# Bilinear blending of a deformable convolution: from rows-then-columns to columns-then-rows, with ScalarE first

## The chip, the core and the metric

The kernel runs on one core of a Trainium2 chip. The metric is the device time of one execution in microseconds (us), and the comparison is of medians. TensorE (PE) multiplies and transposes, its weight loads are listed as PEld; VectorE (DVE) and ScalarE (ACT) work element by element; GpSimd (POOL) issues the gathers; SyncE (SP) issues the other transfers. Each engine takes its own instructions strictly in the order in which they were written for it, and waits for others by semaphores.

## What is computed

The input is x, 4 images of 256 channels of 64 x 64 pixels, in float32. Three deformable 3 x 3 convolutions with ReLU follow each other on a normalised x, the result is added to x, and a mixture of eight experts (two per token) works on the pixels as tokens. The change is in the sampling of the deformable convolution, in the reference:

```
v00 = _gather(feat, y0i, x0i); v01 = _gather(feat, y0i, x1i)
v10 = _gather(feat, y1i, x0i); v11 = _gather(feat, y1i, x1i)
return v00*(1-wy)*(1-wx) + v01*(1-wy)*wx + v10*wy*(1-wx) + v11*wy*wx
...
sampled = _bilinear(x, ys, xs) * mask[:, None]
out = jnp.einsum('bikhw,oik->bohw', sampled, wk) + b[None, :, None, None]
```

Every output pixel takes, for each of 9 taps, four neighbouring pixels (two rows, a left and a right column) of 256 channels, blends them with weights of its own, and multiplies by a 256 x 256 matrix of that tap.

## The kernel before

A table in HBM holds for each position 512 values: the 256 channels of the upper pixel (v) and the 256 differences from it to the lower pixel (d). So `v + wy*d` blends two rows, and two neighbouring positions lie next to each other: one gather of 1024 values per pixel brings the left column (v, d) and the right column (v, d).

The work goes in 12 stages (3 layers x 4 images, interleaved), each of 8 blocks of 512 pixels, each block in 9 taps, each tap in four tiles of 128 pixels: 12 x 8 x 9 x 4 = 3456 tiles. `main_block` (L430) does for each tile:

- gather `g` (L445, POOL), into a ring of `GB` = 10 buffers of 4 KB a partition;
- **D1** (L451, DVE, 512 values): `g.v += wy * g.d`, for both columns, in place;
- **A** (L456, ACT, 256 values): `s = left * cf[1]`, with `s` from a ring of 6;
- **D2** (L461, DVE, 256 values): `s += right * cf[2]`;
- **T** (L465, PE): two transposes of `s` into PSUM. When the two tiles of a pair are transposed, **S** (L470, ACT) copies the pair to `sT`.

In the source the pair is written D1, A, D1, A, D2, D2. After the four tiles, `finish` (L477) issues the products of the tap before (L488, PE, from its `sT`), `step` and `pump` (L870) hand out pieces of other work: storing the table of the next layer (L263), the offset convolution and its plan of positions (L310), normalising (L388), and routing and experts of images that are done (L519 to L842).

The order of instructions on each engine isn't the source's: a scheduler sorts them when the program is built, by its own estimate of what is ready when. Within an engine the order is then fixed. A buffer of `g` is free again when its last reader is done (here D2); the gather that takes it waits for that on POOL, in front of all later gathers.

Of the kernel before, what the change touches and what calls it, by code (L numbers as in the profile page):

```python
# [8 lines left out]
F32 = mybir.dt.float32  # L9
I32 = mybir.dt.int32  # L10
AF = mybir.ActivationFunctionType
ALU = mybir.AluOpType
AX = mybir.AxisListType

P = 128
H = W = 64
C = 256
CC = C // P
K = 9
# [15 lines left out]
FT_LOG = 8  # L35
FT = 1 << FT_LOG
FU = FT // P
GB = 10
WINN = CC * (RPB + 2) * (W + 2)
W1N = CC * HID + HC  # L40
W2N = HC * C + C
# [43 lines left out]
class Weave:  # L85
# [3 lines left out]
    def __init__(self, ctx, tc, ins, out):  # L89
# [7 lines left out]
        def pool(name, bufs, **kw):  # L97
            return ctx.enter_context(tc.tile_pool(name=name, bufs=bufs, **kw))
# [14 lines left out]
        self.smp = pool("smp", 6)  # L113
        self.gat = pool("gat", GB)
        self.ps = pool("ps", 3, space=bass.MemoryType.PSUM)
# [314 lines left out]
    def main_block(self, i, n, wins):  # L430
        nc = self.nc
        l, b = self.stages[i]
        nm = f"{i}_{n}"
        idx, cf = self.plans.pop((l, b, n))
        tb = self.table(l, b)
        acc = self.ps1.tile([P, CC, BLK], F32, tag="acc", name=f"acc_{nm}")
        for k in range(K):
            sT = self.smT.tile([P, CC, BLK], F32, tag="sT", name=f"sT_{nm}_{k}")
            for t0 in range(0, TPB, 2):
                tp = self.ps.tile([P, CC, 2 * P], F32, tag="tp", name=f"tp_{nm}_{k}_{t0}")  # L440
                gs, ss = [], []
                for t in (t0, t0 + 1):
                    j = t * K + k
                    g = self.gat.tile([P, 2, 2, C], F32, tag="g", name=f"g_{nm}_{j}")
                    nc.gpsimd.indirect_dma_start(  # L445
                        out=g.rearrange("p x s f -> p (x s f)"),
                        out_offset=None,
                        in_=tb,
                        in_offset=bass.IndirectOffsetOnAxis(ap=idx[:, j : j + 1], axis=0),
                    )  # L450
                    nc.vector.scalar_tensor_tensor(  # L451
                        g[:, :, 0, :], g[:, :, 1, :], cf[:, j, 0:1], g[:, :, 0, :],
                        ALU.mult, ALU.add,
                    )
                    s = self.smp.tile([P, C], F32, tag="s", name=f"s_{nm}_{j}")
                    nc.scalar.activation(s, g[:, 0, 0, :], AF.Copy, scale=cf[:, j, 1:2])  # L456
                    gs.append(g)
                    ss.append(s)
                for u in range(2):
                    j = (t0 + u) * K + k  # L460
                    nc.vector.scalar_tensor_tensor(  # L461
                        ss[u], gs[u][:, 1, 0, :], cf[:, j, 2:3], ss[u], ALU.mult, ALU.add
                    )
                    for c in range(CC):
                        nc.tensor.transpose(  # L465
                            tp[:, c, u * P : (u + 1) * P],
                            ss[u][:, c * P : (c + 1) * P],
                            self.ident,
                        )
                nc.scalar.copy(sT[:, :, t0 * P : (t0 + 2) * P], tp)  # L470

            self.finish()
            self.pend = (i, n, k, acc, sT, wins)
            self.step(k)
            self.pump()
# [501 lines left out]
```

## Time and profile before

| | us |
|---|---|
| median of 17 runs | 8086.85 (8047.05 to 8119.2) |
| the profiled execution | 8099.05 |
| its span, first to last instruction | 8097.1 |
| PE busy | 6793.9 (84%) |
| DVE busy | 5034.7 (62%) |
| POOL busy | 4519.1 (56%) |
| ACT busy | 3581.9 (44%) |
| transfers of gathered and other indirect data | 1929.26 MB |
| read from HBM and written | 290 GB/s over the span |

The mean granted clock of TensorE is 0.932 of full speed. The first 170 us make the first table (the first gather is at 166.6 us), the convolutions run until about 7515 us, and the last 580 us are experts and sums of the last image. PE's busy time includes overlap that the profile models, so it is not PE at its peak.

In a list of instructions a row gives start, duration, engine, line, operation, result and sources, how many were merged, and in brackets the idle time of the engine before it and what ended it. In a list of waits a row gives the waiting instruction, what it waited for, and the total in us, how many times, the longest. In a table of stretches a row gives, for each of PE, PEld, DVE, ACT and POOL, busy us and instructions, then granted clock, busy share of the DMA engines and GB/s.

### The profile page before, as it was taken

To read this page: it belongs to the slowest core of one execution; us is meant where nothing else is said; L and a number is where in the kernel's file an instruction comes from. 1 tells how busy PE (TensorE), PEld (TensorE's weight loads), DVE (VectorE), ACT (ScalarE), POOL (GpSimd) and SP (SyncE) were. 2 spreads that over 40 slices of the span, in tenths; PEclk is the share of its full clock that TensorE was granted. 3 is DMA by queue.
4 is the path that set the end of the run, shared out by engine and by line. 5 is a ranking of instruction groups with operands and counts; after the bars stand their busy time and mean duration, and the time that the engine had idled before them with its cause. 6 is when DMAs were issued, how large, how long until landed. Compare 5 with 4: busy or idle time off the path is not lost. (4 is left out here: it accounts for less than half of the span.)

```text
span 8097.1 us, 92242 instructions
## 1 busy us (share of the span) xinstructions
PE 6793.9 (84%) x27544; PEld 3720.1 (46%) x27544; DVE 5034.7 (62%) x11300; ACT 3581.9 (44%) x7355; POOL 4519.1 (56%) x4189
## 2 busy tenths in 40 slices
PE   6898888888988989988877899988887787778595
PEld 2444333334444444445533445544444444445374
DVE  4776777778885666666667666666665544556401
ACT  3554544445544444445543444444543333444121
POOL 1665666665655666655555566655555544545434
PEclk8999999999999999999988999999998889889697
DMA  5998999899987888887778888888787666667423
GB/s 154 324 329 283 335 328 320 311 326 335 349 290 275 307 298 302 299 283 276 284 270 277 277 304 294 305 294 288 272 296 233 237 231 223 245 239 276 139 94 117
DMA packets 751193, 2210.66 MB, mean 273 GB/s; under 512 B 105688, under 2 KB 206040, under 8 KB 746088
## 3 DMA queue, kind: packets, MB, share of 16 engines
q0 software_dynamic: 547392, 1929.26, 68.0%
q1 hardware_dynamic: 203304, 275.51, 10.1%
q8 instruction: 222, 3.64, 0.2%
q14 instruction: 275, 2.25, 0.1%
HBM read 2150.57 MB, written 195.61 MB: 290 GB/s over the span
## 5 line engine op out<-in xcount | busy, mean ns | idle before, releaser
L445 POOL DMA_INDIRECT g<-tab,idx x3456 | 3735.8, 1081 | 2474.8 <-DVE s L461 1274.9
L488 PE MATMUL acc<-sT,wk 128*128 128x512 f32 x6912 | 3503.8, 626 | 286.2 <-ACT sT L470 161.8
L461 DVE SCALAR_TENSOR_TENSOR s<-g,cf,s 128x256 f32<-128x256 f32 x3456 | 1625.0, 482 | 1751.0 <-ACT s L456 1306.3
L451 DVE SCALAR_TENSOR_TENSOR g<-g,cf 128x512 f32<-128x512 f32 x3456 | 2520.6, 745 | 235.1 <-DMA g<-tab,idx 193.9
L456 ACT ACTIVATE s<-g,cf 128x256 f32<-128x256 f32 x3456 | 1691.1, 509 | 1172.9 <-DVE g L451 895.6
L488 PEld LDWEIGHTS acc<-sT,wk 128*128 128x128 f32 x6912 | 1218.5, 199 | 1298.8 <-issue 940.5
L470 ACT COPY sT<-tp 128x512 f32<-128x512 f32 x1728 | 1002.4, 584 | 1747.2 <-PE tp L465 1196.3
L465 PE MATMUL tp<-ident,s 128*128 128x128 f32 x6912 | 1306.1, 287 | 427.8 <-DVE s L461 280.0
L465 PEld LDWEIGHTS tp<-ident,s 128*128 128x128 f32 x6912 | 878.9, 146 | 1664.5 <-issue 1014.5
L791 PE MATMUL py<-w,hT 128*128 128x256 f32 x2496 | 693.5, 400 | 139.0 <-ACT hT L785 99.9
L775 PE MATMUL ph<-fzT,w 128*128 128x256 f32 x2496 | 675.1, 401 | 68.0 <-ACT hT L785 26.4
L791 PEld LDWEIGHTS py<-w,hT 128*128 128x128 f32 x2496 | 449.6, 196 | 288.2 <-ACT hT L785 150.2
L727 POOL DMA_INDIRECT w<-in_W,wrow x156 | 174.8, 1121 | 723.7 <-issue 292.4
L775 PEld LDWEIGHTS ph<-fzT,w 128*128 128x128 f32 x2496 | 470.7, 200 | 195.8 <-issue 85.2
L321 PE MATMUL po<-win,wo 128*32 128x512 f32 x2304 | 469.1, 617 | 53.1 <-ACT win L256 31.3
L785 ACT ACTIVATE hT<-ph,w 128x256 f32<-128x256 f32 x624 | 268.3, 471 | 547.4 <-PE ph L775 285.2
L739 POOL DMA_INDIRECT zt<-z,tok x312 | 348.3, 1116 | 140.7 <-issue 87.2
L820 POOL DMA_INDIRECT gy<-ys,slots x256 | 258.9, 1011 | 228.4 <-DVE ta L828 117.2
L799 DVE TENSOR_TENSOR y<-py,w 128x512 f32<-128x512 f32 x156 | 107.5, 689 | 345.7 <-PE py L791 315.4
L291 ACT COPY hv<-tpv 128x512 f32<-128x512 f32 x384 | 211.1, 595 | 110.3 <-PE tpv L286 54.1
L321 PE MATMUL po<-win_pre,wo 128*32 128x512 f32 x1152 | 228.0, 632 | 19.0 <-ACT om L330 7.5
L828 DVE SCALAR_TENSOR_TENSOR ta<-gy,cw,ta 128x256 f32<-128x256 f32 x256 | 121.0, 483 | 121.6 <-DMA gy<-ys,slots 80.6
(151 smaller groups left out, 3644.8 us busy)
## 6 DMA issues: line engine op xcount, KB each, us to landing
tab<-hv SPq DMA_DIRECT2D x384, 256.0 KB
g<-tab,idx POOLq DMA_INDIRECT x3456
ys<-y SPq DMA_DIRECT2D x156, 256.0 KB
wk<-in_conv_w SPq DMA_DIRECT2D x108, 256.0 KB
xc_pre<-in_x SPq DMA_DIRECT2D x32, 512.0 KB
xr_tok<-in_x SPq DMA_DIRECT2D x32, 512.0 KB
t<-t_tok SPq DMA_DIRECT2D x32, 512.0 KB
ta<-t SPq DMA_DIRECT2D x64, 256.0 KB
```

What stands on the lines that cost most here:

```text
L321: nc.tensor.matmul(po[g * Q : (g + 1) * Q, :], lhsT=self.wo[l][:, k, c, :], rhs=w[:, c, ky : ky + RPB, kx : kx + W], start=(m < NQ), stop= ...
L445: nc.gpsimd.indirect_dma_start(out=g.rearrange("p x s f -> p (x s f)"), out_offset=None, in_=tb, in_offset=bass.IndirectOffsetOnAxis(ap=id ...
L451: nc.vector.scalar_tensor_tensor(g[:, :, 0, :], g[:, :, 1, :], cf[:, j, 0:1], g[:, :, 0, :], ALU.mult, ALU.add,)
L456: nc.scalar.activation(s, g[:, 0, 0, :], AF.Copy, scale=cf[:, j, 1:2])
L461: nc.vector.scalar_tensor_tensor(ss[u], gs[u][:, 1, 0, :], cf[:, j, 2:3], ss[u], ALU.mult, ALU.add)
L465: nc.tensor.transpose(tp[:, c, u * P : (u + 1) * P], ss[u][:, c * P : (c + 1) * P], self.ident,)
L470: nc.scalar.copy(sT[:, :, t0 * P : (t0 + 2) * P], tp)
L488: nc.tensor.matmul(acc[:, o, :], lhsT=self.wk[k][:, c, o * P : (o + 1) * P], rhs=sT[:, c, :], start=(k == 0 and c == 0), stop=(k == K - 1 ...
L739: self.nc.gpsimd.indirect_dma_start(out=zt, out_offset=None, in_=grp.zd, in_offset=bass.IndirectOffsetOnAxis(ap=grp.tok[:, j : j + 1], axi ...
L775: nc.tensor.matmul(ph[:, h, :], lhsT=w1[:, o : o + P], rhs=zT[:, c, :], start=(c == 0), stop=(c == CC - 1),)
L785: nc.scalar.activation(ht[:, h, :], ph[:, h, :], AF.Gelu, bias=w1[:, k : k + 1])
L791: nc.tensor.matmul(py[:, u, :], lhsT=hT[h // 2][:, h % 2, u * P : (u + 1) * P], rhs=w2[:, h * C : (h + 1) * C], start=(h == 0), stop=(h == ...
```

## The change

The order of blending is turned around. ACT scales the whole left column (v and d, 512 values) straight from the gathered data. DVE adds the right column (512 values) and then, directly on its own result, blends the rows (256 values). Per tile there are still one ACT and two DVE instructions. The order in the source is now A, D1, D2 for one tile, then for the next. `s` has 512 values a partition in place of 256 (6 buffers of 2 KB in place of 1 KB), and `GB` goes from 10 to 9. The last reader of `g` is now D1. The gather, the transposes, the copies and the products are the same.

```diff
-GB = 10
+GB = 9
...
-                gs, ss = [], []
-                for t in (t0, t0 + 1):
-                    j = t * K + k
-                    g = self.gat.tile([P, 2, 2, C], F32, tag="g", name=f"g_{nm}_{j}")
+                for u in range(2):
+                    j = (t0 + u) * K + k
+                    g = self.gat.tile([P, 2, 2 * C], F32, tag="g", name=f"g_{nm}_{j}")
...
+                    s = self.smp.tile([P, 2 * C], F32, tag="s", name=f"s_{nm}_{j}")
+                    nc.scalar.activation(s, g[:, 0, :], AF.Copy, scale=cf[:, j, 1:2])
                     nc.vector.scalar_tensor_tensor(
-                        g[:, :, 0, :], g[:, :, 1, :], cf[:, j, 0:1], g[:, :, 0, :],
-                        ALU.mult, ALU.add,
+                        s, g[:, 1, :], cf[:, j, 2:3], s, ALU.mult, ALU.add
                     )
-                    s = self.smp.tile([P, C], F32, tag="s", name=f"s_{nm}_{j}")
-                    nc.scalar.activation(s, g[:, 0, 0, :], AF.Copy, scale=cf[:, j, 1:2])
-                    gs.append(g)
-                    ss.append(s)
-                for u in range(2):
-                    j = (t0 + u) * K + k
                     nc.vector.scalar_tensor_tensor(
-                        ss[u], gs[u][:, 1, 0, :], cf[:, j, 2:3], ss[u], ALU.mult, ALU.add
+                        s[:, :C], s[:, C:], cf[:, j, 0:1], s[:, :C], ALU.mult, ALU.add
                     )
```

More of the change, by code (lines that the diff above doesn't have):

```diff
@@ L440, in main_block @@
                 tp = self.ps.tile([P, CC, 2 * P], F32, tag="tp", name=f"tp_{nm}_{k}_{t0}")
-                gs, ss = [], []
-                for t in (t0, t0 + 1):
-                    j = t * K + k
-                    g = self.gat.tile([P, 2, 2, C], F32, tag="g", name=f"g_{nm}_{j}")
+                for u in range(2):
+                    j = (t0 + u) * K + k
+                    g = self.gat.tile([P, 2, 2 * C], F32, tag="g", name=f"g_{nm}_{j}")
                     nc.gpsimd.indirect_dma_start(
-                        out=g.rearrange("p x s f -> p (x s f)"),
+                        out=g.rearrange("p x f -> p (x f)"),
                         out_offset=None,
@@ L465, in main_block @@
                         nc.tensor.transpose(
-                            tp[:, c, u * P : (u + 1) * P],
-                            ss[u][:, c * P : (c + 1) * P],
-                            self.ident,
+                            tp[:, c, u * P : (u + 1) * P], s[:, c * P : (c + 1) * P], self.ident
                         )
```

## Prediction

> **What bounds the kernel now.** I read the page's busy times first: PE 84%, DVE 62%, ACT 44%, so PE is nearest to the end, though not at it. The table of stretches tells whether that holds everywhere. A row of the early convolutions and one of the stages with experts beside them:
>
> ```profile
> 800.00:1200.00 400.00, 344.02 (x1341) 157.66 (x1342) 291.99 (x582) 199.63 (x412) 259.52 (x236) 1.00 0.93 330
> 4800.00:5200.00 400.00, 369.26 (x1494) 202.13 (x1493) 257.09 (x522) 188.86 (x400) 251.29 (x227) 0.97 0.84 292
> ```
>
> PE is 86% and 92% busy, DVE 73% and 64%, the DMA engines 93% and 84%. No resource is full; the rest is engines waiting for each other in turn. The list of waits says who:
>
> ```profile
> DVE s L461 <- ACT s L456: 1306.3, 1254, 15.9
> POOL g L445 <- DVE s L461: 1274.9, 1036, 10.3
> ACT sT L470 <- PE tp L465: 1196.3, 952, 6.2
> ACT s L456 <- DVE g L451: 895.6, 910, 8.7
> ...
> PEld tp L465 <- DVE s L461: 372.3, 547, 6.5
> ...
> DVE g L451 <- DMA g<-tab,idx: 193.9, 103, 9.1
> ```
>
> DVE waits for A, A for D1, the copy S for the transposes T, T for D2, and gathers for a free buffer. D1 seldom waits for data: 103 times in 3456, so gathers are ahead of their use. The durations of the ring come from the list of instructions. Early on, with one tile after the other:
>
> ```profile
> 999.80 0.48 DVE L461 SCALAR_TENSOR_TENSOR s<-g,cf,s 128x256 f32<-128x256 f32 x1
> ...
> 1000.20 0.74 DVE L451 SCALAR_TENSOR_TENSOR g<-g,cf 128x512 f32<-128x512 f32 x1
> ...
> 1000.98 0.51 ACT L456 ACTIVATE s<-g,cf 128x256 f32<-128x256 f32 x1 [1.22 <-DVE g L451]
> ...
> 1001.52 0.48 DVE L461 SCALAR_TENSOR_TENSOR s<-g,cf,s 128x256 f32<-128x256 f32 x1 [0.58 <-ACT s L456]
> ```
>
> From D2 to the next D1 0.40 us, D1 to A 0.78, A to D2 0.54: 1.72 us a tile, 3.44 a pair, in strict turns, with DVE idle 0.58 of it. Elsewhere the copy is in the way:
>
> ```profile
> 3001.56 0.49 DVE L461 SCALAR_TENSOR_TENSOR s<-g,cf,s 128x256 f32<-128x256 f32 x1 [0.58 <-ACT s L456]
> 3001.97 1.41 DVE L451 SCALAR_TENSOR_TENSOR g<-g,cf 128x512 f32<-128x512 f32 x2
> ...
> 3002.11 0.44 PE L465 MATMUL tp<-ident,s 128*128 128x128 f32 x2 [0.42 <-DVE s L461]
> ...
> 3002.58 0.58 ACT L470 COPY sT<-tp 128x512 f32<-128x512 f32 x1 [1.05 <-issue]
> 3003.06 0.91 ACT L456 ACTIVATE s<-g,cf 128x256 f32<-128x256 f32 x2
> ...
> 3003.61 0.88 DVE L461 SCALAR_TENSOR_TENSOR s<-g,cf,s 128x256 f32<-128x256 f32 x2 [0.23 <-ACT s L456]
> ```
>
> D2 to T 0.55, T to S 0.47, S to the next A 0.48, a second A 0.40 behind (0.91 - 0.51), A to D2 0.55. Both D1 ran meanwhile (second 0.67 behind the first, 1.41 - 0.74). So this pair took 0.55 + 0.47 + 0.48 + 0.40 + 0.55 = 2.45 us, and its D1 cost nothing.
>
> How much of the time is this ring? I followed the chain of waits back, by the page's rule, from a point every 130 us between 740 and 7510 us: it covers 6656 us, of which PE has 3749, D1 276, A 218, D2 204, S 123. Those four are 821 us. With some 35 us of handovers (about 700 of them at 0.05) and 75 us of transposes between D2 and S (160 at 0.47), about **930 us** of the path is the ring. The rest is mostly PE.
>
> **The change, part by part.**
>
> *ACT.* 3456 A of 256 become 512 values. The trace has no such A from SBUF. Biased ACTIVATEs from PSUM take 687 ns for 512 (L330) and 471 for 256 (L785), 216 more; plain copies of 512 take 584. Bounds: 584 and 725 (509 + 216). I take 0.72 us, since the form is an ACTIVATE: 3456 x 0.21 = 726 us more on ACT, 3582 to some 4310 (53%). Beside PE this is hidden; in the ring it counts.
>
> *DVE.* D1 and D2 keep sizes and forms (745 and 482 ns), so busy time stays near 5035. But D2 now waits for D1 on its own engine. Independent instructions overlap: D2 to D1 is 0.40 though D2 lasts 0.48. Dependent ones don't:
>
> ```profile
> 1011.99 0.20 DVE L363 TENSOR_SCALAR pos<-pos 128x72 f32<-128x72 f32 x1
> ...
> 1012.23 0.27 DVE L365 CAST pi<-pos 128x72 int32<-128x72 f32 x1
> ```
>
> The second starts 0.04 after the first has ended. So D1 to D2 is 0.745 + 0.04 = 0.79 us, and not 0.67: DVE alone needs 2 x (0.79 + 0.40) = 2.38 us a pair, before 2 x (0.67 + 0.40) = 2.14. The Trainium skill, "VectorE: DVE Perf Modes", section "The DRAIN you can't avoid", speaks otherwise: chaining with semaphores took the same time as without, so the semaphore costs nothing extra. By it, D1 to D2 stays 0.67, and the ring reckoned below would be 2.74 us a pair in place of 2.92; the rows here overlap only where nothing is awaited, so I keep 0.79.
>
> *The ring.* Before, D1 ran ahead of A whenever ACT was held up by S. Now D1 and D2 both stand behind A. What matters is how many of a pair's A stand in ACT's fixed order before the S of the pair before. I counted it in the orders of both builds (1727 pairs). Before: none 865, one 701, both 161. After: none 162, one 931, both 634. So the scheduler moves A ahead by about one tile.
>
> Before, by DVE's order as well: 643 pairs with both A behind S and both D1 ahead of D2, 2.45 us; 482 in strict turns, 3.44; the other 602 held by DVE alone, 2.14. Mean: (1575 + 1658 + 1288) / 1727 = **2.62 us a pair**.
> After, with one A behind S: D2 to T 0.55, S 0.47, A 0.48, D1 0.76 (0.72 + 0.04), D2 0.79: 3.05. With both behind, 0.40 + 0.79 more: 4.24. With none, DVE alone: 2.38. Mean: (931 x 3.05 + 162 x 4.24 + 634 x 2.38) / 1727 = **2.92 us a pair**, 11.5% more.
>
> The strict turns go, which is the change's gain, but the longer way behind each S outweighs it. If the ring set the pace throughout, that would be 1727 x 0.30 = 518 us; at the 930 us that it holds of the path, 930 x 0.115 = **107 us**. I take the latter, since PE holds 56% of the path. The lower end is a gain, priced as the first rival.
>
> *Buffers.* One gather fewer ahead is one tile's period, about 2.1 us (7340 us / 3456), whenever the reserve runs out, at most 103 times: 216 us. Against it, `g` comes free at D1 in place of D2, so below zero is possible by up to 0.79 us at the same 103 times, -81. I take **20 us**, nearer to zero, because the two partly cancel. POOL has the same 3456 gathers; behind a gather that waits stand further gathers, expert weights (L727) and token rows (L739), and behind these PE's products of L775 and L791.
>
> *PE, S, SP.* The same instructions; their places change with the scheduler. On PE the transposes of single tiles lie more evenly among the products (9592 runs of equal instructions in place of 9373). I price it at nothing: PE has work to do meanwhile. Should that cover fail, each of 1727 pairs could wait one more transpose pair, 0.2 us: up to 345 us.
>
> **Sum.** 8099 + 107 + 20 = 8226 for the profiled execution. The median stands 12 us below that execution, so I forecast **8214 us**, 1.6% slower.
>
> **The rivals.**
> 1. *Faster: the handover was the pace.* DVE's 1306 us of waiting for A vanish, because A needs landed data alone and gathers are ahead. For it: strict turns make 1.72 us a tile, and the tiles of 740 to 1740 us come every 1.70 to 1.77. Price: at least the 136 steps from D1 to A on the walked path at 0.55, 75 us; at most all 218 us of A and these 75, 293. Middle -184: 7903; span 7794 to 8012. It decides when A stays two tiles ahead of S nearly always, so that DVE runs through. Against it: in the built order that holds for 634 of 1727 pairs.
> 2. *Slower throughout: the ring sets the pace.* Most pairs have exactly one A ahead, each then takes 3.05 us, and PE's idle time grows in the stages with experts too. Price 518 us: 8605 by the median. Against it: those stages need over 4 us a pair already (8097 us / 1727 = 4.7), mostly PE's.
> 3. *No change.* PE and the transfers (93% busy early on) hide both sides: 8087. It needs a balance within 16 us.
>
> **How the numbers follow.** Forecast 0.47 (8103 to 8450), rival 1 0.32 and a smaller gain within it, rival 2 0.12, rival 3 0.09. A measurement of this kernel can tell about 0.2%, 16 us, from no change. So faster 0.32, same 0.09, slower 0.59. The range leaves out the far half of rival 1, below 7900, and most of rival 2, above 8480: **7900 to 8480**. The forecast's own range is 8103 to 8450.
>
> **What would show it.** A at 0.70 to 0.74 us, and ACT near 4310 busy; outside that the ACT step is wrong. "DVE <- ACT" at D1 should remain a long wait, 1000 us or more; under rival 1 it falls below 400. S waiting for T should grow with DVE between; D2 starts 0.79 after D1, or 0.67 if the skill's rule holds. D1 or A waiting for gathers should stay under 300 us in all; much more means that the tenth buffer mattered. A walked path with less of D1, A, D2 than 700 us makes the ring step wrong.

## The result, and the profile after the change

The changed kernel takes 8273.08 us (median of 8 runs, 8261.46 to 8295.28) against 8086.97 us (47 runs): a ratio of **1.0237 [1.0222, 1.0252]**, 186 us slower. The forecast was 8214 us.

The profiled execution spans 8262.4 us (before: 8097.1), at a mean granted clock of 0.927 (before: 0.932). The page's busy times:

```profile
PE 6811.8 (82%) x27544; PEld 3723.9 (45%) x27544; DVE 5142.6 (62%) x11300; ACT 4204.3 (51%) x7355; POOL 4403.9 (53%) x4189
```

ACT has 622 us more work and DVE 108 us more; PE has the same work and is idle for longer. The table of stretches, in the columns and the two places that the prediction shows:

```profile
800.00:1200.00 400.00, 327.85 (x1278) 149.59 (x1279) 286.90 (x555) 230.88 (x398) 238.27 (x228) 1.00 0.89 315
4800.00:5200.00 400.00, 351.33 (x1379) 186.67 (x1377) 249.19 (x481) 209.31 (x372) 221.41 (x215) 0.95 0.82 281
```

In 400 us PE does 1278 matmuls in place of 1341 early, and 1379 in place of 1494 in the stage with experts beside it: 5% and 8% less, at nearly the same clock. The same stretch of time doesn't hold quite the same work in the two kernels, so these shares overstate the loss; but it is not in the early stages alone. Cut at the first copy S of a stage and at the end of the last S, the profiled executions give (us):

| | stages 1 to 4 | stages 5 to 12 | after the last S |
|---|---|---|---|
| before | 2084 | 5257 | 581 |
| after | 2121 | 5387 | 579 |
| difference | +37 (1.8%) | +130 (2.5%) | -2 |

The experts' first products come at 2453 us in the kernel before and at 2501 in the changed one, in stage 5. The list of waits of the changed kernel (D1 is now L453, A L452, D2 L456, T L460, S L463):

```profile
ACT sT L463 <- PE tp L460: 1492.2, 1047, 6.7
DVE s L453 <- ACT s L452: 1430.3, 804, 20.9
POOL g L444 <- DVE s L453: 1430.1, 846, 8.6
...
PEld tp L460 <- DVE s L456: 527.2, 647, 6.3
...
ACT s L452 <- DMA g<-tab,idx: 185.8, 111, 9.2
...
DVE s L453 <- DMA g<-tab,idx: 109.1, 29, 8.9
```

The wait of D2 for A (1306.3) has become a wait of D1 for A (1430.3), seldomer and longer; the wait of A for D1 (895.6) is gone. In their place S waits longer for the transposes (1196.3 to 1492.2), and the weight loads of the transposes for D2 (372.3 to 527.2). What these waits look like can be read in a piece of the list of instructions:

```profile
1008.64 0.38 PE L460 MATMUL tp<-ident,s 128*128 128x128 f32 x2
...
1009.22 0.59 ACT L463 COPY sT<-tp 128x512 f32<-128x512 f32 x1 [2.58 <-PE tp L460]
...
1009.70 1.34 ACT L452 ACTIVATE s<-g,cf 128x512 f32<-128x512 f32 x2
...
1010.46 0.75 DVE L453 SCALAR_TENSOR_TENSOR s<-g,cf,s 128x512 f32<-128x512 f32 x1 [2.50 <-ACT s L452]
...
1011.25 0.48 DVE L456 SCALAR_TENSOR_TENSOR s<-s,cf 128x256 f32<-128x256 f32 x1
...
1011.65 0.75 DVE L453 SCALAR_TENSOR_TENSOR s<-g,cf,s 128x512 f32<-128x512 f32 x1
...
1011.79 0.44 PE L460 MATMUL tp<-ident,s 128*128 128x128 f32 x2
...
1012.26 0.58 ACT L463 COPY sT<-tp 128x512 f32<-128x512 f32 x1 [1.23 <-PE tp L460]
```

ACT stands 2.58 us in front of S, with two A queued behind it (the second tile of the next pair and the first tile of the pair after that), though neither then waits for its gathered data: their gathers were issued some 15 us earlier. DVE, which needs the first A, has nothing to do for 2.50 us; then come D1, D2 (0.79 behind D1), T and the next S: 3.04 us from S to S. That is the prediction's ring with an A behind S, 3.05 us.

### The profile page after: what moved, and what is told of

Same layout as the page of the kernel before. It is cut to its first block, busy times and chain, and to the rows that moved or that the text cites. A ratio compares the mean times of both kernels' runs of the same rounds, so it can differ in the third digit from the quotient of the medians.

```text
span 8262.4 us, 93641 instructions
## 1 busy us (share of the span) xinstructions
PE 6811.8 (82%) x27544; PEld 3723.9 (45%) x27544; DVE 5142.6 (62%) x11300; ACT 4204.3 (51%) x7355; POOL 4403.9 (53%) x4189
## 5 line engine op out<-in xcount | busy, mean ns | idle before, releaser
L444 POOL DMA_INDIRECT g<-tab,idx x3456 | 3650.6, 1056 | 2753.8 <-DVE s L453 1430.1
L453 DVE SCALAR_TENSOR_TENSOR s<-g,cf,s 128x512 f32<-128x512 f32 x3456 | 2559.0, 748 | 1983.7 <-ACT s L452 1430.3
L481 PE MATMUL acc<-sT,wk 128*128 128x512 f32 x6912 | 3553.4, 629 | 280.3 <-ACT sT L463 168.4
L452 ACT ACTIVATE s<-g,cf 128x512 f32<-128x512 f32 x3456 | 2354.7, 721 | 311.1 <-DMA g<-tab,idx 185.8
L463 ACT COPY sT<-tp 128x512 f32<-128x512 f32 x1728 | 1008.2, 585 | 2119.7 <-PE tp L460 1492.2
L481 PEld LDWEIGHTS acc<-sT,wk 128*128 128x128 f32 x6912 | 1217.1, 201 | 1199.1 <-issue 836.7
L460 PE MATMUL tp<-ident,s 128*128 128x128 f32 x6912 | 1346.4, 288 | 454.8 <-DVE s L456 307.9
L456 DVE SCALAR_TENSOR_TENSOR s<-s,cf 128x256 f32<-128x256 f32 x3456 | 1638.7, 482 | 108.7 <-issue 31.8
L460 PEld LDWEIGHTS tp<-ident,s 128*128 128x128 f32 x6912 | 888.2, 146 | 1807.1 <-issue 930.2
L732 POOL DMA_INDIRECT zt<-z,tok x312 | 327.7, 1050 | 140.1 <-issue 89.6
L827 PE MATMUL otp<-ident,ta 128*128 128x128 f32 x256 | 70.8, 377 | 185.9 <-issue 121.9
```

Source lines behind the costliest of these rows:

```text
L444: nc.gpsimd.indirect_dma_start(out=g.rearrange("p x f -> p (x f)"), out_offset=None, in_=tb, in_offset=bass.IndirectOffsetOnAxis(ap=idx[:, ...
L452: nc.scalar.activation(s, g[:, 0, :], AF.Copy, scale=cf[:, j, 1:2])
L453: nc.vector.scalar_tensor_tensor(s, g[:, 1, :], cf[:, j, 2:3], s, ALU.mult, ALU.add)
L456: nc.vector.scalar_tensor_tensor(s[:, :C], s[:, C:], cf[:, j, 0:1], s[:, :C], ALU.mult, ALU.add)
L460: nc.tensor.transpose(tp[:, c, u * P : (u + 1) * P], s[:, c * P : (c + 1) * P], self.ident)
L481: nc.tensor.matmul(acc[:, o, :], lhsT=self.wk[k][:, c, o * P : (o + 1) * P], rhs=sT[:, c, :], start=(k == 0 and c == 0), stop=(k == K - 1 ...
```

## The experiments

The theories at the start. **Ring**: A stands behind S in ACT's fixed order, and D1 and D2 both behind A; the place of A decides. **Long A**: ACT's 512 values by themselves cost the time. **Buffers**: the tenth gather buffer is missed. The runs came in three visits, and the kernel before took 7965, 7487 and 8076 us there; so each ratio is to the kernel before of the same visit, and ratios of different visits are compared with care.

"Pairs with both A ahead" means, as in the prediction, that both A of a pair stand in ACT's order before the S of the pair before: 161 of 1727 in the kernel before, 634 in the changed one.

### First visit: each suspect alone

**The kernel before with nine buffers.**

```diff
-GB = 10
+GB = 9
```

> The kernel before with 9 gather buffers in place of 10, nothing else. Before is 8087 us, after 8273. Ring theory (the loss is D1 standing behind A, behind the copy S): the tenth buffer is worth little, 8080 to 8130. Buffer theory (the loss is the shorter reserve of gathers): 8190 to 8270. Long-A theory (the loss is ACT's 726 us more): 8087, plus or minus 15.

Measured: 7896.24 us, **0.9925 [0.9896, 0.9953]**. No theory had the sign: nine buffers are better than ten in the old order. Its list of waits, to be read against the lines of before in the prediction:

```profile
...
DVE s L461 <- ACT s L456: 1186.7, 1279, 18.4
...
DVE g L451 <- DMA g<-tab,idx: 193.8, 133, 8.8
```

D1 waits for gathered data 193.8 us with nine buffers and, in the profile of the first result, 193.9 with ten: by this view the tenth bought no data. Why nine are faster is open; the order on the engines is nearly the same (161 pairs with both A ahead become 159). So the lost buffer does no harm in the old order. The changed kernel with ten buffers was not run, so for the new order this isn't shown.

**The same, with a long A.** ACT scales 512 values of `g`, of which the second half is not used.

```diff
-GB = 10
+GB = 9
...
-                    s = self.smp.tile([P, C], F32, tag="s", name=f"s_{nm}_{j}")
-                    nc.scalar.activation(s, g[:, 0, 0, :], AF.Copy, scale=cf[:, j, 1:2])
+                    s = self.smp.tile([P, 2 * C], F32, tag="s", name=f"s_{nm}_{j}")
+                    nc.scalar.activation(s, g[:, 0, :, :].rearrange("p s f -> p (s f)"), AF.Copy, scale=cf[:, j, 1:2])
...
```

> The kernel before with 9 gather buffers, and A over the left column's 512 values (blended values and differences; the second half of s isn't used), so A is as long as after the change, but D1 still stands ahead of A. Ring theory: A of 0.72 us costs only where A is on the ring, 0.21 us on some 471 pieces of the walked path at most, up to 100 us: 8090 to 8190. Long-A theory: all of the loss, 8250 to 8290. Buffer theory: as with 9 buffers alone, 8190 to 8270.

Measured: 7946.14 us, **0.9983 [0.9959, 1.0006]**, below every expectation, but 0.6% above the run before, which has the same nine buffers and an A of 256 values. The group of A shows that the work was there:

```profile
L456 ACT ACTIVATE s<-g,cf 128x512 f32<-128x512 f32 x3456 | 2406.7, 722 | 782.6 <-DVE g L451 428.3 <-issue 223.4 <-ACT s L456 56.7
```

A is busy 2406.7 us, in the run before 1693.3: 713 us more on ACT cost about 50 us of the kernel, where the order of D1, A, D2 is the old one. That is a net figure, since the scheduler also moved A: 1319 of 1727 pairs have at least one A ahead of S, 860 in the run before (both ahead: 214 and 159). By the ring theory that helps, so the long A by itself may cost more. In the old order it is far from the whole loss; for the new order this run says nothing.

**The new order with a short A.** ACT scales v of the left column alone, D1 works in place on `g` and adds that to both halves, and D2 blends; `g` is then held until D2, with ten buffers. This kernel leaves out the left column's differences, so its values, and with them the positions that the second and third layer gather and the choice of experts, aren't those of the other kernels. The diff is against the changed kernel.

```diff
-GB = 9
+GB = 10
...
-                    nc.scalar.activation(s, g[:, 0, :], AF.Copy, scale=cf[:, j, 1:2])
+                    nc.scalar.activation(s, g[:, 0, :C], AF.Copy, scale=cf[:, j, 1:2])
                     nc.vector.scalar_tensor_tensor(
-                        s, g[:, 1, :], cf[:, j, 2:3], s, ALU.mult, ALU.add
+                        g[:, 1, :].rearrange("p (s f) -> p s f", s=2),
+                        g[:, 1, :].rearrange("p (s f) -> p s f", s=2),
+                        cf[:, j, 2:3], s.unsqueeze(1).to_broadcast([P, 2, C]),
+                        ALU.mult, ALU.add,
                     )
                     nc.vector.scalar_tensor_tensor(
-                        s[:, :C], s[:, C:], cf[:, j, 0:1], s[:, :C], ALU.mult, ALU.add
+                        s, g[:, 1, C:], cf[:, j, 0:1], g[:, 1, :C], ALU.mult, ALU.add
                     )
```

> The new order with a short A: A scales 256 values (the left column's differences are left out), D1 adds the right column's 512 values to it in place in g, D2 blends the rows from g into s. 10 buffers, s of 256. So D1 stands behind A, but A is short and the buffers are as before. Ring theory: one A behind the copy gives 2.84 us a pair in place of 3.05, most of the loss stays: 8170 to 8260. Long-A theory and buffer theory: the loss is gone, 8070 to 8120.

Measured: 8362.96 us, **1.0504 [1.0464, 1.0544]**. Long A and buffers both wanted this kernel near the old time, and it is the slowest of all. The ring theory had the sign and missed the size. What is late is again the way from A to S:

```profile
ACT sT L466 <- PE tp L463: 1879.1, 1050, 7.6
DVE g L453 <- ACT s L452: 1315.2, 859, 13.7
```

With 508 pairs with both A ahead, in place of 634, it stands further back by the ring's measure, though its A is shorter. That goes with the loss, but isn't isolated: the longer hold of `g`, the write in place and the other positions came with it.

**The changed kernel, with A put ahead of S.** An edge that orders without a semaphore tells the scheduler to issue S only after both A of the next pair (within a block of pixels). Nothing else in the source changes.

```diff
+        held = None
...
+                scaled = []
...
-                    nc.scalar.activation(s, g[:, 0, :], AF.Copy, scale=cf[:, j, 1:2])
+                    scaled.append(
+                        nc.scalar.activation(s, g[:, 0, :], AF.Copy, scale=cf[:, j, 1:2]).ins
+                    )
...
-                nc.scalar.copy(sT[:, :, t0 * P : (t0 + 2) * P], tp)
+                if held is not None:
+                    for a in scaled:
+                        self.tc.add_manual_dep(
+                            held,
+                            a.name,
+                            mybir.DependencyInfo(
+                                mybir.DependencyClass.NoSync, mybir.DependencyReason.DATA
+                            ),
+                            reason="scale ahead of the copy",
+                        )
+                held = nc.scalar.copy(sT[:, :, t0 * P : (t0 + 2) * P], tp).ins
```

> The kernel after, with an edge for the scheduler alone (no wait on the chip): on ACT the copy S of a pair is issued after both A of the next pair in the block. 1643 of 1727 pairs then have both A ahead (634 before the edge). Ring theory: a pair falls from 2.92 to some 2.4 us, 18% of the 964 us that the ring now holds of the walked path, 170 us: 8050 to 8150. Long-A and buffer theories: nothing changes, 8260 to 8290, since ACT has the same work and the buffers are the same.

Measured: 7986.10 us, **1.0025 [1.0006, 1.0045]**, with 1643 pairs with both A ahead. That is inside the range of the ring theory. The buffers, the long A and the instructions are those of the changed kernel, and the time is nearly that of before: the place of A in ACT's order, with what the scheduler moves along with it, is worth about 2%. It does move more: 1789 of PE's 27544 instructions stand over 20 places from where they stood in the changed kernel, and 606 of DVE's 11300 over three places. No run separates these moves from the place of A. The changed kernel itself was not run in that visit, so it was taken up again below.

### Second visit: the edge in other kernels

**The changed kernel again**, with no edit.

> The kernel after, unchanged, for the same chip as the next ones, since times differ from chip to chip by over 1%. All theories: a ratio to the kernel before of 1.020 to 1.028, as measured first (1.0237).

Measured: 7558.96 us, **1.0089 [1.0070, 1.0107]**, well under the first ratio and the expectation. Here everything was faster (before 7487.41). The last section shows what was different.

**The short A with the edge**: the edit of the short A and that of the edge together, ten buffers.

> The new order with the short A (left column's differences left out, 10 buffers, g held until D2), which was 1.050 times the time before, now with both A of the next pair issued ahead of S (1640 of 1727 pairs, 508 without the edge). Ring theory: a pair then goes at DVE's own 2.38 us, whatever A's length, so the ratio is that of the same edge with the long A (1.0025): 0.995 to 1.012. If instead the excess of the short A is in its buffers (g held longer, written in place), the edge leaves at least 1.02.

Measured: 7237.47 us, **0.9672 [0.9656, 0.9688]**, below every expectation. The ring theory held that the length of A no longer matters once both A stand ahead of S. But with the long A the same edge gives 1.0025 in the first visit and 1.0011 in the third, over 3% more. So either the long A has a price in the new order that the missing edge hides, or the tenth buffer, the write in place or the left-out part of the blend has it. Other positions aren't the whole of it: in the four stages of the first layer, whose positions come from x alone, this kernel takes 2019 us and the changed kernel of this visit 2171. Which of the rest it is, no run shows.

**The short A with nine buffers**, without the edge. The diff is against the first kernel with the short A.

```diff
-GB = 10
+GB = 9
```

> The new order with the short A, 9 gather buffers in place of 10, no edge. In the old order the ninth instead of the tenth buffer gave 0.9925. If buffers explain why the short A is slower than the long one (10 against 9), 1.02 to 1.03; if they have no part in it, 1.04 to 1.055.

Measured: 7601.64 us, **1.0159 [1.0140, 1.0178]**, below both ranges. They were reckoned from ratios of the first visit, and the changed kernel fell in this one too (1.0237 to 1.0089), so what the ninth or tenth buffer does here stays open. The run is 0.6% above the changed kernel of this visit: a shorter A doesn't help while it stands behind S (506 pairs with both ahead). Between this run and the one before it lie the edge and one buffer, and 364 us.

**The kernel before with the edge**: `scaled` and `held` as above, ten buffers.

> The kernel before (old order, 10 buffers) with the same edge: on ACT, S of a pair after both A of the next pair (1634 of 1727 pairs, 161 without). Ring theory: D1 then has to stand ahead of S as well; a pair falls from 2.62 to some 2.2 us, 15% of some 930 us on the path, 140 us: ratio 0.975 to 0.99, which would beat both kernels. If A behind S isn't what costs time, 1.00 or more, because S is delayed by A.

Measured: 7395.53 us, **0.9877 [0.9854, 0.9899]**, as the ring theory had it. The old order has A behind S too, and gains from the same remedy. The edge is thus not a remedy for the change alone, and what it gives back to the changed kernel is not all the change's own loss.

### Third visit: the few tenths, on one chip

**The kernel before again**, with no edit.

> The kernel before, unchanged, for a profile on the same chip as the next three. All theories: a ratio of 1.00.

Measured: 8070.62 us, **0.9990 [0.9973, 1.0007]**: what a kernel without a difference gives.

**The changed kernel again.**

> The kernel after, unchanged, on that chip. Two chips gave 1.0237 and 1.0089. Where the waits that the profile puts down to nothing (issue) are as long as in the first two profiles, some 1.02 to 1.028; where they are short, 1.006 to 1.012.

Measured: 8251.32 us, **1.0215 [1.0200, 1.0231]**: the first result stands.

**The changed kernel with the edge again.**

> The kernel after with S held behind both A of the next pair, now beside the kernel after on one chip. Ring theory: 1.5% to 4% below the kernel after, and D1's waits for A below it too. If ACT's longer work were the cost, no more than 0.5% below the kernel after.

Measured: 8081.67 us, **1.0011 [0.9998, 1.0024]**: 170 us less than without the edge, on the same chip. Its list of waits:

```profile
...
ACT sT L477 <- PE tp L464: 1002.9, 732, 6.4
DVE s L457 <- ACT s L455: 993.7, 461, 20.1
...
PEld tp L464 <- DVE s L460: 288.9, 516, 5.1
```

Without the edge these waits were 1544.6, 1497.2 and 552.8 us in this visit; all three steps of the ring shrink together. In the list of instructions at the same place as above:

```profile
1004.24 0.59 ACT L477 COPY sT<-tp 128x512 f32<-128x512 f32 x1 [0.60 <-PE tp L464]
1004.40 0.49 DVE L460 SCALAR_TENSOR_TENSOR s<-s,cf 128x256 f32<-128x256 f32 x1
...
1004.72 1.33 ACT L455 ACTIVATE s<-g,cf 128x512 f32<-128x512 f32 x2
1004.80 0.75 DVE L457 SCALAR_TENSOR_TENSOR s<-g,cf,s 128x512 f32<-128x512 f32 x1
...
1005.59 0.48 DVE L460 SCALAR_TENSOR_TENSOR s<-s,cf 128x256 f32<-128x256 f32 x1
...
1005.99 0.75 DVE L457 SCALAR_TENSOR_TENSOR s<-g,cf,s 128x512 f32<-128x512 f32 x1
```

DVE starts D1 at 1004.80, while the two A behind S have only begun (1004.72): it works on a tile scaled before S. From D1 to D1 1.19 us, and no row of DVE has an idle time before it.

**The kernel before with the edge and nine buffers.**

> The kernel before with the same edge and 9 buffers. The edge alone gave 0.9877, 9 buffers alone 0.9925, on different chips. If the two add, 0.975 to 0.985; it should then beat both kernels. In the old order D1 must now run ahead of S on a second round trip between ACT and DVE, so ring theory expects the new order with the edge to come out at least level with it.

Measured: 7911.83 us, **0.9788 [0.9771, 0.9805]**: 2.1% faster than the kernel before, and it beats both kernels. That the new order with the edge would come out at least level with it was wrong: the new order takes 2.1% longer (8081.67 against 7911.83), with the edge and nine buffers in both. In the new order with the edge S still waits 1002.9 us for the transposes. In the old one that wait has nearly gone, but A, which stands ahead of S there, waits for D1 instead:

```profile
ACT s L459 <- DVE g L453: 1556.4, 1598, 8.7
...
ACT sT L484 <- PE tp L469: 193.7, 186, 4.7
```

The stages of the profiled executions of this visit:

| us | stages 1 to 4 | stages 5 to 12 |
|---|---|---|
| before | 2079 | 5260 |
| after | 2126 | 5404 |
| after, with the edge | 2017 | 5280 |
| before, with the edge and nine buffers | 2043 | 5088 |

In the first four stages the new order with the edge is the fastest of all, 26 us below the old one with the edge. It loses its 192 us in the stages that have experts beside them. These are single executions: that of the kernel before is 28 us above its median, that of the changed kernel 34 above, that with the edge 26 below and that of the last row 24 below.

## Why the prediction was right, and where it wasn't

The sign was right, and the way that the prediction named is there: D1, D2 and T stand behind A, A stands behind S, and with A put ahead of S 170 of 175 us went on one chip (8251 to 8082, the kernel before 8076). That does not make the place of A the whole of what divides the two orders. The same edge takes 1.2% off the old order too, and with the edge and nine buffers in both the new order still takes 2.1% longer. The prediction compared the orders mostly by the place of A. For pairs with both A ahead it has 2.38 us against 2.14 where DVE alone sets the pace, since D2 waits for D1; whether that is what is left, no run isolates. And that 8214 lies only 59 us below the measured 8273 is in part luck, since one of its two terms had the wrong sign where it was measured. By its own steps:

*ACT.* Predicted 0.72 us for A and 4310 us busy. Measured, in the groups of instructions:

```profile
L453 DVE SCALAR_TENSOR_TENSOR s<-g,cf,s 128x512 f32<-128x512 f32 x3456 | 2559.0, 748 | 1983.7 <-ACT s L452 1430.3 <-issue 288.0 <-DMA g<-tab,idx 109.1
L452 ACT ACTIVATE s<-g,cf 128x512 f32<-128x512 f32 x3456 | 2354.7, 721 | 311.1 <-DMA g<-tab,idx 185.8 <-PE tp L460 85.7 <-issue 26.1
L456 DVE SCALAR_TENSOR_TENSOR s<-s,cf 128x256 f32<-128x256 f32 x3456 | 1638.7, 482 | 108.7 <-issue 31.8 <-DMA g<-tab,idx 5.1 <-DVE s L453 3.9
```

721 ns, right. ACT is busy 4204 us in place of 4310. 62 us of that come from A that follow each other and overlap (two take 1.34 us, not 1.44), the rest lies in ACT's other work. The prediction priced the work beside PE at nothing; the long A in the old order cost about 50 us net, and with the edge the kernel with the short A is over 3% below that with the long one, for a reason that is not isolated.

*DVE.* D1 and D2 keep their durations (748 and 482 ns); DVE is busy 5143 us in place of 5035. A D2 that directly follows the D1 of its own tile starts 0.786 us after it (median of 1940); one that directly follows the D1 of another tile starts 0.662 us after it (332, in the same trace). Predicted 0.79. So the wait of an instruction for the one ahead of it on its own engine takes away the overlap, 0.12 us a tile. The Trainium skill, "VectorE: DVE Perf Modes", section "The DRAIN you can't avoid", reports that a row of eight copies took as long with a semaphore after each as without. That doesn't carry over to this pair, and the prediction read the section as wider than it is. It also says that a next instruction that isn't held starts earlier, which agrees with the 0.662 us here. What these 0.12 us cost the kernel was not isolated.

*The ring.* Its parts were right: D1 starts 0.76 us after A where it waits for it (predicted 0.76), the next D1 0.401 after D2 (0.40), and the stretch shown above takes 3.04 us from S to S (3.05). D1, A, D2 and S grew on the walked path as foreseen, from 821 to some 960 us (in the third visit from 810 to 931, and 738 with the edge); D1, A and D2 have over 800 of it, above the 700 below which the step would have been wrong. But **107 us was too little, and the reason given against more was wrong.** The prediction held that the stages with experts would hardly feel the ring, since a pair takes over 4 us there and mostly by PE's work. They lost 2.5%, more than the early ones (1.8%), and with the edge the profiled executions got back 124 us there and 109 in the early ones. The walked path doesn't show that. Behind 2240 us the four steps take some 570 us of it before and as much after (in the third visit 577 and 583), while between 740 and 2240 us they grow from 251 to 352, in stages that lost 37. Under which name the late loss stands on the path is open: issue grew (616 to 676 us in the third visit, and 593 with the edge), and the products of L481 grew in the first profiles (1361 to 1417) but not in the third visit (1367 and 1365). So the share of the path places the loss badly, though its sum came near.

*Buffers.* Predicted +20 us, for a tenth buffer that is missed at D1's waits for data. In the old order nine buffers made it 0.75% faster. In the changed kernel A and D1 wait for gathers 295 us in all (185.8 + 109.1), under the 300 set as a limit; before it was 234 (193.9 + 39.9), so the 61 us between are the most that this view gives a missed buffer. The term had the wrong sign in the only place where it was measured; if the same held in the new order, the rest of the change would cost 250 us, not 186. That is not shown.

*PE.* Priced at nothing, with 345 us if its cover failed. In the trace the transposes stand in 2838 runs among the products, before in 2603. With the edge there are still 2838, and the time is back at the old; with the edge and the old order there are 2562. So this number doesn't explain the 170 us. The edge did move PE's instructions otherwise, and whether their places make part of the 170 us, or of the 2.1% between the two kernels with the edge, is open.

*Rival 1*, that the handover was the pace, fails for the changed kernel: D1's wait for A is 1430 us, not below 400. Where its condition was met, A two tiles ahead in 1643 of 1727 pairs, the time was 1.0011 of before, not 75 to 293 us below, and D1 still waited 994 us for A; 62 us of the gain show in the first four stages (2079 to 2017), and 20 are lost again in the others. But with the short A and the edge the time was 250 us below before (7237 against 7487), which is in the rival's price. So its gain is not refuted for every kernel of the new order, though the one that had it leaves out part of the blend. *Rival 2* wanted 518 us and PE idle with experts beside: the place was right, the size a third. *Rival 3* fell with the first result.

**Open.** Why nine buffers beat ten. Why the short A is slower than the long one as long as A stands behind S (1.0159 against 1.0089). What part of the edge's 170 us the scheduler's other moves have. And what holds the new order 2.1% behind the old one when both have the edge and nine buffers: in the profiles it is lost in the stages with experts, and S waits 1003 us for the transposes in the one and 194 in the other, where A waits 1556 us for D1. The long A may have part of it: about 50 us net in the old order, and possibly more in the new one, as the run of the short A with the edge suggests. It also fits that D1 and D2 now both stand behind ACT, so that DVE has no work left when ACT does the experts' (in the old order D1 needs gathered data alone); no run isolates that.

## What to carry to other kernels

Before an operation is moved ahead of another engine's, look at what stands in front of it in its own engine's fixed order: here a copy that waits for the end of the same ring, and moving A in front of it gave 2.1% in the changed kernel and 1.2% in the old one, for no instruction more. Try such a remedy on the kernel before as well: only then is it seen how much of the loss is the change's own, and here 2.1% remained. An operation that needs landed data alone may be better placed on the engine that would otherwise run dry; taking that role from DVE made DVE depend on ACT for everything, which fits the 2.1% but isn't shown to cause them. And a ring is not to be priced by its share of the path alone: here the stages that PE seemed to fill lost more than the early ones, while the ring's share of their path didn't grow.

## What was not expected of the hardware

The same kernel took 8087, 7965, 7487 and 8076 us in four visits, within about 1% in each. The changed kernel was 1.0237 and 1.0215 of it at 8087 and 8076, but 1.0089 at 7487. In that visit the waits look different:

```profile
ACT sT L463 <- PE tp L460: 1696.6, 1273, 8.6
DVE s L453 <- ACT s L452: 1365.7, 1094, 10.4
...
PEld acc L481 <- issue: 679.0, 2664, 0.8
```

The waits of the ring are as large as ever, but the longest wait of a weight load for nothing that the profile shows is 0.8 us. In the first profile of the changed kernel it is this:

```profile
PEld acc L481 <- issue: 836.7, 2760, 10.0
```

The same holds for D1: its idle time put down to nothing is 288.0 us in 190 cases there, and 0.6 us in 2 here. Counted over all engines but POOL, up to the last S, idle times of more than 2 us that the profile puts down to nothing are 260 in the first profile of the changed kernel, 968 us in all, and 46 here, 182 us. In the four profiles of this visit they are 36 to 46, in the ten others 182 to 285. The granted clock was 0.957 here against 0.927. So in some visits the engines stand still now and then for 2 us and more, for a reason that the profile doesn't name, and where they do, the changed kernel lost 103 to 115 us more than where they don't. That a chain in which each engine waits for the next suffers more from such stops is a guess. Their sum alone doesn't set the time: in the third visit it is 955 us in the changed kernel and 1023 with the edge, which is 170 us faster. What they are wasn't found.
